# Moving the query and key transposes one unit ahead, and one mask ahead of an eviction, in a fused transformer block

## The chip, the cores and the metric

The kernel runs on one core of a Trainium2 chip. The metric is the time of one execution on the device in microseconds (us); the median of 14 runs of the kernel before is 694.04 us. A profile of one execution stands beside it. Engines are named as the profile does: PE (TensorE, matmuls and transposes), DVE (VectorE), ACT (ScalarE), POOL (GpSimd, here mostly indirect transfers), SP (SyncE, plain transfers).

## The reference

Input x has 8 sequences of 512 tokens with 128 features, all float32. Three residual steps follow each other:

```python
x = x + 0.5 * ffn(layernorm(x))     # 8 experts, 128 -> 512 -> 128, relu, the best 2 of 8 per token
x = x + attention(layernorm(x))     # 16 heads of 8, causal, rotary on some heads, decay on some
x = x + 0.5 * ffn(layernorm(x))     # the same weights again
```

Inside the attention, with q and k already rotated where a head's type asks for it:

```python
scores = einsum('bhqd,bhkd->bhqk', q, k) * dh ** (-0.5) + decay + causal
out    = einsum('bhqk,bhkd->bhqd', softmax(scores), v) @ w_o
```

## The kernel before

**Groups and units.** The attention is cut into 96 units, numbered 0 to 95: 8 sequences, each with 4 groups of 4 heads, each group with 3 units (`STEPS`, line 1227) that take key tiles 0; 1; and 2 with 3. Unit n therefore belongs to sequence n // 12, and n % 12 is its place there. In the trace, unit n begins with the n-th set of `st` matmuls (line 1238). The first attention unit starts at 143.4 us and the last at 558.9 us. Units below 0 and from 96 on carry only expert work and routing.

**What a unit does**, in `surround` (from line 1465), which writes the order out by hand for PE, ACT, DVE and SP:

1. `scores(n)`: PE computes the transposed scores of 4 heads into `st` (one PSUM buffer of four banks), and ACT takes the exponential in two halves of two heads each, `ee` (line 1245). The second `scores` can't begin before both halves of the one before are read.
2. `values(n - 1)`: PE multiplies the `ee` of the unit before with the values into `o` (line 1264). After a group's third unit ACT copies `o` to `oT`.
3. The first piece of expert work (below).
4. `causal(…, 0)`: DVE applies the mask to the first half of `ee` (line 1252), as a minimum with a tile that holds zeros and a very large number.
5. One queued transfer on POOL (`transfer`).
6. `outputs` in a group's second unit after the first group has ended: PE transposes `oT`, DVE takes the reciprocal of the sums (`recs`, line 1286) and writes `o_tok` (line 1287).
7. `causal(…, 1)`: the mask on the second half.
8. What is due in this unit (below), with further pieces between, then additions and a second transfer.

**Expert work.** Groups of tokens f0, f1, f2 (first expert step) and g0, g1, g2 (second) run beside the attention. A piece is one of three: a transpose of gathered rows (`xbT`, line 1000), a first layer part (`z`, line 1013, eviction to `h` at lines 1020 or 1022), or a second layer part (`y`, line 1037, eviction at line 1041, always DVE). A quota of one to three pieces goes into each unit. `m.evac` says which engine evicts the first piece of a unit if it is a transpose or a first layer part: DVE, but ACT in the places 8, 9 and 10 of a sequence, where DVE does the rotary work and writes `qpad` and `kpad` for the next sequence (lines 1193 to 1205). Later pieces of a unit are evicted by ACT.

**PSUM.** In the attention stage `st` and `o` have their own banks, and all else (pieces, transposes of queries, keys, outputs, normalised rows, qkv, routing) shares three banks called `m`: a new tile on PE waits until the old one in its bank is evicted.

**What is due.** `at(u, stream, steps)` puts steps of a generator into units u, u + 1, and so on; within a unit, they run in the order in which they were entered. For a sequence b that starts at unit u = 12 b:

- `operands(b, g)` has two steps. The first transposes the padded queries of group g (`qT_ps`, 4 transposes on PE) and copies them on DVE (`qT`). The second does the same for the keys (`kT_ps`), with the copy on ACT (`kT`, line 1221). `qT` and `kT` have two buffers each.
- `project(b + 1)` works in places 2 to 9 of sequence b: normalise (2 to 4), transpose (5), qkv matmuls with ACT's copies (6 and 7, lines 1176 to 1180), rotary (8), and `qpad`/`kpad` (9). So the first group's operands of the next sequence can't come before place 10.
- `finish(b)` and `route` of the sequence before come in places 2, 3 and from 4 on; `route` normalises in place 6 (line 774), transposes in 7 and computes the logits in 8.

**Transfers.** Scatters and gathers wait in a list; each, when issued on POOL, waits for the instruction that was last written down in `self.mark`: the latest mask of `causal` (line 1256) or the latest eviction of a first or second layer part (lines 1023 and 1044). The adds that use gathered rows are put two units after the gather (line 1120).

Of the kernel before, what the change touches and what calls it, by code (L numbers as in the profile page):

```python
# [1340 lines left out]
def macaron_kernel(  # L1341
# [24 lines left out]
    def run(*streams):  # L1366
        for s in streams:
            for _ in s:
                pass
# [12 lines left out]
    def take(stream, n):  # L1382

        for _ in range(n):
            if next(stream, STOP) is STOP:
                return
            yield
# [5 lines left out]
    with ExitStack() as main:  # L1393
        m = Main(tc, main, aps)
# [17 lines left out]
        def close(g):  # L1412
            m.close_group(g, order.index(g))

        def opened(g):

            pieces = m.experts(g)
            next(pieces)
            return pieces

        def step(*streams):
            for st in streams:
                next(st, None)

        def transfers(n):
            for _ in range(n):
                m.transfer()
# [4 lines left out]
        units = [(b, g, s) for b in range(B) for g in range(G) for s in range(len(m.STEPS))]  # L1432
        per = len(m.STEPS)
# [4 lines left out]
        def at(u, stream, steps, each=1):  # L1438

            for k in range(steps):  # L1440
                due.setdefault(u + k // each, []).append((stream, 1))

        def routed(u, shares, urgent=False, ahead=False):
            early = u < 0 or u > core
            r = m.route(shares, urgent, ahead, early)
            steps = 7 if early else 8
            if u > core:
                at(u, r, 3 + steps, 3)
                return
            if shares[0][0] is not f1:  # L1450
                at(u, r, 3)
                u += 3
            at(u, r, steps)

        def combined(u, g, i, dst=None, urgent=False, ahead=False):
            at(u, m.combine(g, i, dst, urgent, ahead), 1)
# [8 lines left out]
        def surround(n, att):  # L1465

            m.unit = n
            now = None
            for g, fetch, start, end in plan:
                if n == fetch:  # L1470
                    close(g)
                    fills[g.key] = [opened(g), g.pieces]
                if n == end:
                    run(fills[g.key][0])
                if start <= n < end:
                    now, until = fills[g.key], end
                    if g is g1 and att:
                        until = end + 7
            quota = min(now[1], -(-now[1] // (until - n))) if now else 0
            fill = now[0] if now else iter(())  # L1480
            if now:
                now[1] -= quota
            if att:
                ee = m.scores(*units[n])
            last, m.oT = m.oT, None
            if m.held is not None:
                got = m.values(*m.held)
                if got is not None:
                    m.oT = (*m.held[:2], got)
            m.held = (*units[n], ee) if att else None  # L1490
            m.evac = "dve" if att and n % seq not in (8, 9, 10) else "act"
            run(take(fill, 1 if quota else 0))
            m.evac = "act"
            if att:
                m.causal(units[n][2], ee, 0)
            m.transfer()
            if last is not None:
                m.outputs(*last)
            if att:
                m.causal(units[n][2], ee, 1)  # L1500
            if not att:
                m.additions()
            work = due.pop(n, [])
            todo = max(quota - 1, 0)
            for k, (stream, steps) in enumerate(work):
                some = todo // (len(work) - k + 1)
                run(take(stream, steps))
                run(take(fill, some))
                todo -= some
            if n >= core and len(m.jobs) + len(m.results) > 2:  # L1510
                run(take(fill, todo // 2))
                todo -= todo // 2
                m.transfer(second=True)
            run(take(fill, todo))
            m.additions()
            m.transfer(second=True)

        m.held = m.oT = None
        with m.banks(("m", 8)):

            n = [m.normalise(b) for b in range(5)]
            r = [m.route([(f0, 0)], early=True), m.route([(f0, 1)], early=True),
                 m.route([(f1, 0)], True, early=True)]
            step(n[0], n[0], n[1], n[1], n[0], n[0])
            step(r[0], n[1], n[1], r[0], r[1], r[0], r[0])
            transfers(8)
            step(r[1], r[1], r[1], n[2], n[2])
            transfers(8)
            step(n[3], n[3], n[4], n[4], *[r[0], r[1]] * 3, n[2], n[2])
            step(r[2], r[2], r[2], n[3], n[4], n[3], n[4])  # L1530
            run(*r[:2], *n)
            m.bias_columns()

            at(first, r[2], 4)
            routed(first + 1, [(f1, 1)], urgent=True)
            routed(first + 3, [(f1, 2)], urgent=True)
            routed(-22, [(f2, 0)], urgent=True)
            combined(-16, f0, 0, urgent=True, ahead=True)
            routed(-14, [(f2, 1)], urgent=True)
            combined(-12, f0, 1, urgent=True)  # L1540
            routed(-10, [(f2, 2)], urgent=True)
            at(-10, m.project(0), 8)
            for b in range(B):
                u = b * seq
                if b == 2:
                    combined(7, f1, 0, urgent=True, ahead=True)
                elif b > 2:
                    combined(u - (17 if b == 5 else 21), *place[True][b][0], urgent=b == 5, ahead=b == 5)
                if b > 0:
                    at(u - 10, m.project(b), 8)  # L1550
                for g in range(G):
                    at(u + g * per - 2, m.operands(b, g), 2)
                at(u + seq + 2, m.finish(b), 2, 2 if b == B - 1 else 1)
                routed(u + seq + (3 if b == B - 1 else 4), place[False][b], urgent=b in (1, 4, 5, 6, 7), ahead=b in (4, 6, 7))
            for i in range(2):
                combined(79 + 7 * i, g0, i, out)
            for i, (_, t0, t1) in enumerate(g1.shares):
                at(tail + 2 + 3 * i, m.collect(g1, i, out), 1 + t1 - t0)
            at(tail, m.verdict(bad), 2)

            for u in range(first, 0):
                surround(u, False)
                if u == first:
                    m.attention_constants()
                for _ in range(min(2, len(m.loads))):
                    m.loads.popleft()()
        with m.banks(("st", 1), ("o", 1), ("m", 3)):
            for u in range(core + 2):
                surround(u, u < core)
                if u >= 12 and m.later:  # L1570
                    m.later.popleft()()
        with m.banks(("m", 8)):
            for u in range(core + 2, ends):
                surround(u, False)
            run(fills["g2"][0])
            assert not due, due
            assert not m.jobs and not m.adds
            while m.results:
                m.transfer()
            last = [m.collect(g2, i, out, parts=min(2, g2.shares[i][2] - g2.shares[i][1])) for i in range(4)]  # L1580
            step(*last)
            run(*last)
# [53 lines left out]
```

## Time and profile before

| | |
|---|---|
| median of 14 runs | 694.04 us (691.68 to 695.62) |
| the profiled execution | 695.35 us, of which the span from first to last instruction is 693.6 us |
| mean granted TensorE clock | 0.978 |
| busy: PE, DVE, ACT, POOL | 623.1, 404.1, 347.2, 295.7 us |
| PE busy, 150 to 550 us, in stretches of 50 us | 50.00, 50.00, 49.51, 49.88, 48.58, 48.82, 46.58, 49.50 us |
| granted clock, 580 to 600 and 600 to 620 us | 0.83 and 0.83; 1.00 from 20 to 580 us |
| PE's longest waits outside the stage | for gathered rows, 9.9 us near the start; 3.4 us at 609.4 us |

In a timeline row the columns are start, length, engine, line, operation, output and input, shapes and count; a bracket gives how long the engine was idle just before, and whose work ended that. In a row of waits they are who waited for whom, the sum, how often, and the longest. PE's ends are modelled, so a wait is better read from the starts of the neighbours.

### The profile page before, as it was taken

To read this page: it belongs to the slowest core of one execution; us is meant where nothing else is said; L and a number is where in the kernel's file an instruction comes from. 1 tells how busy PE (TensorE), PEld (TensorE's weight loads), DVE (VectorE), ACT (ScalarE), POOL (GpSimd) and SP (SyncE) were. 2 spreads that over 40 slices of the span, in tenths; PEclk is the share of its full clock that TensorE was granted. 3 is DMA by queue.
4 is the path that set the end of the run, shared out by engine and by line. 5 is a ranking of instruction groups with operands and counts; after the bars stand their busy time and mean duration, and the time that the engine had idled before them with its cause. 6 is when DMAs were issued, how large, how long until landed. Compare 5 with 4: busy or idle time off the path is not lost. (4 is left out here: it accounts for less than half of the span.)

```text
span 693.6 us, 12921 instructions
## 1 busy us (share of the span) xinstructions
PE 623.1 (90%) x4797; PEld 403.5 (58%) x4797; DVE 404.1 (58%) x1426; ACT 347.2 (50%) x564; POOL 295.7 (43%) x318
## 2 busy tenths in 40 slices
PE   3259999999999999999999999999999998989980
PEld 2148867666556556555656656455565656747760
DVE  6736438735466665675676677777666554333423
ACT  4034443454755665466466565566646542234422
POOL 3744637643222214324054324342244556665550
PEclk9999999999999999999999999999999998989995
DMA  8746843313409941101211101012102121144225
GB/s 270 192 136 193 225 115 100 85 49 78 100 20 167 225 144 42 27 20 47 67 32 51 46 25 39 27 36 81 47 29 62 32 62 39 42 143 143 77 66 158
DMA packets 80230, 61.33 MB, mean 88 GB/s; under 512 B 7400, under 2 KB 73888, under 8 KB 80160
## 3 DMA queue, kind: packets, MB, share of 16 engines
q1 hardware_dynamic: 71296, 42.79, 24.0%
q0 software_dynamic: 8576, 17.63, 8.3%
q8 instruction: 40, 0.66, 0.4%
q14 instruction: 30, 0.25, 0.1%
q10 hardware_dynamic: 288, 0.01, 0.0%
HBM read 26.21 MB, written 34.19 MB: 87 GB/s over the span
## 5 line engine op out<-in xcount | busy, mean ns | idle before, releaser
L1245 ACT ACTIVATE ee<-st 128x768 f32<-128x768 f32 (+1 forms) x192 | 159.0, 881 | 90.5 <-PE st L1238 85.2
L479 POOL DMA_INDIRECT yt_f<-ys,back_f x64 | 65.1, 1018 | 128.7 <-DVE ee L1252 55.9
L1252 DVE TENSOR_TENSOR ee<-ee,keep 128x256 f32<-128x256 f32 (+1 forms) x192 | 93.2, 507 | 22.2 <-ACT ee L1245 21.9
L1037 PEld LDWEIGHTS y_f<-w_sb,h_f 128*120 128x120 f32 (+1 forms) x704 | 85.8, 182 | 28.5 <-issue 16.2
L1238 PE MATMUL st<-qT,kT 32*128 32x512 f32 (+3 forms) x1024 | 96.1, 467 | 5.7 <-ACT kT L1221 3.3
L1037 PEld LDWEIGHTS y_g<-w_sb,h_g 128*128 128x128 f32 x640 | 81.7, 193 | 32.5 <-issue 25.7
L895 POOL DMA_INDIRECT xs<-xn_g,to_g x64 | 63.8, 997 | 85.7 <-DVE ee L1252 32.5
L1037 PE MATMUL y_f<-w_sb,h_f 128*120 128x128 f32 (+1 forms) x704 | 93.9, 277 | 0.2 <-DVE h_f L1022 0.2
L1013 PE MATMUL z_g<-xT_g,w_sb 128*128 128x512 f32 (+1 forms) x192 | 91.0, 561 | 1.4 <-ACT xT_g L1004 1.4
L1264 PE MATMUL o<-ee,vpad 128*32 128x512 f32 (+3 forms) x1024 | 89.6, 442 | 0.8 <-DVE ee L1252 0.8
L1013 PE MATMUL z_f<-xT_f,w_sb 128*128 128x480 f32 (+1 forms) x192 | 88.9, 552 | 1.0 <-ACT xT_f L1004 1.0
L1020 ACT ACTIVATE h_f<-z_f,b1T 128x480 f32<-128x480 f32 (+1 forms) x86 | 53.5, 623 | 68.3 <-PE z_f L1013 67.4
L1037 PE MATMUL y_g<-w_sb,h_g 128*128 128x128 f32 x640 | 86.3, 280 | 0.5 <-DVE o_tok L1287 0.3
L981 POOL DMA_INDIRECT ys<-ysb_g,home_g x64 | 62.9, 983 | 51.6 <-ACT h_g L1020 17.0
L1020 ACT ACTIVATE h_g<-z_g,b1T 128x512 f32<-128x512 f32 (+1 forms) x77 | 49.4, 643 | 55.5 <-PE z_g L1013 55.3
L1041 DVE TENSOR_TENSOR ysb_f<-y_f,b_sb 120x128 f32<-120x128 f32 (+1 forms) x88 | 25.1, 288 | 77.7 <-PE y_f L1037 74.1
L1041 DVE TENSOR_TENSOR ysb_g<-y_g,b_sb 128x128 f32<-128x128 f32 x80 | 23.1, 290 | 79.4 <-PE y_g L1037 75.5
L1238 PEld LDWEIGHTS st<-qT,kT 32*128 32x128 f32 x1024 | 43.1, 183 | 39.0 <-ACT kT L1221 11.4
L895 POOL DMA_INDIRECT xs<-xn_n,to_f x40 | 39.1, 978 | 35.4 <-ACT xi_sb L732 8.3
L1264 PEld LDWEIGHTS o<-ee,vpad 128*32 128x32 f32 x1024 | 23.7, 108 | 52.5 <-issue 5.5
L1013 PEld LDWEIGHTS z_g<-xT_g,w_sb 128*128 128x128 f32 x192 | 30.5, 197 | 21.7 <-issue 12.5
L1013 PEld LDWEIGHTS z_f<-xT_f,w_sb 128*128 128x128 f32 x192 | 30.3, 194 | 13.9 <-issue 7.2
(187 smaller groups left out, 772.2 us busy)
## 6 DMA issues: line engine op xcount, KB each, us to landing
xs<-zeros SPq DMA_DIRECT2D x8, 520.0 KB
xb_g<-xs SPq DMA_DIRECT2D x16, 260.0 KB
w_sb<-in_L_ffn_W_dram SPq DMA_DIRECT2D x16, 256.0 KB
xb_f<-xs SPq DMA_DIRECT2D x16, 240.0 KB
ys<-ysb_f SPq DMA_DIRECT2D x16, 240.0 KB
ys<-zeros SPq DMA_DIRECT2D x2, 1664.0 KB
x<-in_L_attn_x_dram SPq DMA_DIRECT2D x8, 256.0 KB
xs<-zeros SPq DMA_DIRECT2D x1, 1920.0 KB
```

The costliest lines, as they stand in the source:

```text
L479: ins = op(*args, **kw)
L895: ins = nc.gpsimd.indirect_dma_start(out=g.xs[:, :], out_offset=bass.IndirectOffsetOnAxis(ap=to[:, t, r : r + 1], axis=0), in_=xn[:, t, : ...
L981: ins = nc.gpsimd.indirect_dma_start(out=g.ys[:, :], out_offset=bass.IndirectOffsetOnAxis(ap=home[e][:rows, t : t + 1], axis=0), in_=ys[:r ...
L1013: nc.tensor.matmul(z[:, :n], self.w1_sb[:, e, ts(c, P)], xT[:, n0 : n0 + n], start=True, stop=True,)
L1020: ins = nc.scalar.activation(dst, z[:, :n], AF.Relu, bias=bias)
L1037: nc.tensor.matmul(y[:rows], h[:, c, ts(t, rows)], self.w2_sb[:, e, c, :], start=(c == 0), stop=(c == C - 1),)
L1041: ins = nc.vector.tensor_tensor(ys[:rows, t, :], y[:rows], self.b2_sb[:rows, e], ALU.add)
L1238: nc.tensor.matmul(st[:, h, c0 : c0 + N - kt * P], kT[r0 : r0 + SLOT, ts(kt, P)], qT[r0 : r0 + SLOT, kt * P :], start=True, stop=True,)
L1245: nc.scalar.activation(ee[:, two, :width], st[:, two, :width], AF.Exp)
L1252: ins = self.nc.vector.tensor_tensor(d, d, self.keep.unsqueeze(1).unsqueeze(1).to_broadcast([P, 2, len(parts), P]), ALU.min,)
L1264: self.nc.tensor.matmul(self.o[h * SLOT : (h + 1) * SLOT, kt * P :], self.vpads[b % 2][:, kt, 4 * g + h, :], ee[:, h, c0 : c0 + n], start= ...
```

## The change

Two edits. In a sequence's groups 1 to 3 the operands are entered one unit ahead: queries in unit u + 3 g - 3 (the first unit of the group before) and keys in u + 3 g - 2 (its second), where they stood in the second and the third. The first group stays where it is. And the mask on the first half of `ee` is entered ahead of the first piece instead of behind it, so on DVE it stands in front of that piece's eviction; for the transfer that follows, the piece's eviction (if it sets the mark) is now the later mark.

```diff
             m.held = (*units[n], ee) if att else None
             m.evac = "dve" if att and n % seq not in (8, 9, 10) else "act"
+            if att:
+                m.causal(units[n][2], ee, 0)
             run(take(fill, 1 if quota else 0))
             m.evac = "act"
-            if att:
-                m.causal(units[n][2], ee, 0)
             m.transfer()
...
                 for g in range(G):
-                    at(u + g * per - 2, m.operands(b, g), 2)
+                    at(u + g * per - (3 if g else 2), m.operands(b, g), 2)
```

## The prediction

> **What bounds the kernel now.** I read the page's busy shares first, then PE's waits inside the attention stage (143 to 562 us, 96 units), then PE's, ACT's and DVE's timelines around those waits.
>
> The page's first part, and PE's waits between 143 and 562 us with one line of ACT's (us in total, times, longest):
>
> ```profile
> PE 623.1 (90%) x4797; PEld 403.5 (58%) x4797; DVE 404.1 (58%) x1426; ACT 347.2 (50%) x564; POOL 295.7 (43%) x318
> ...
> PE st L1238 <- ACT kT L1221: 3.3, 8, 0.7
> PE st L1238 <- ACT ee L1245: 1.5, 3, 0.6
> PE qkv_ps_a L1176 <- DVE o_tok L1287: 1.4, 4, 0.7
> ...
> ACT ee L1245 <- PE st L1238: 85.2, 85, 4.3
> ```
>
> PE sets the pace: ACT waits for PE's scores 85 times, while PE waits for others a few us in all. So only what shortens PE's waits counts. The view's own waits are measured from modelled matmul ends; I therefore size a wait from starts: the time from the start of one group of matmuls to the start of the next, less the smallest such time for the same pair (four transposes take 0.44). The kT wait, unit 69, and the exponential wait behind it, PE then ACT:
>
> ```profile
> 446.00 0.63 PE L1215 MATMUL kT_ps<-ident,kpad 128*128 128x128 f32 x4
> 447.31 1.14 PE L1238 MATMUL st<-qT,kT 32*128 32x512 f32 x8 [0.68 <-ACT kT L1221]
> 448.38 0.86 PE L1264 MATMUL o<-ee,vpad 128*32 128x256 f32 x16
> 449.17 0.70 PE L1013 MATMUL z_g<-xT_g,w_sb 128*128 128x256 f32 x2
> 450.51 0.93 PE L1238 MATMUL st<-qT,kT 32*128 32x384 f32 x8 [0.64 <-ACT ee L1245]
> ...
> 446.67 0.59 ACT L1221 COPY kT<-kT_ps 128x512 f32<-128x512 f32 x1 [1.61 <-PE kT_ps L1215]
> 448.52 1.94 ACT L1245 ACTIVATE ee<-st 128x1024 f32<-128x1024 f32 x2 [1.26 <-PE st L1238]
> ```
>
> Transposes at 446.00, copy from 446.67 to 447.26, scores at 447.31: 1.31 us where 0.44 would do, so 0.87 lost.
>
> **Keys and queries sooner.** Nothing is added: 24 groups' two sets of transposes (0.44 each on PE), the qT copy on DVE (0.68) and the kT copy on ACT (0.59) move one unit ahead; no DMA moves. Read from starts, scores wait for kT seven times in groups 1 to 3: 0.30 (st at 350.24), 0.36 (372.88), 0.30 (399.81), 0.40 (432.98), 0.87 (447.31), 0.89 (468.91), 0.21 (480.01), together **3.33 gained**. The waits of first groups (0.42, 0.30, 0.87 at 361.31, 410.89, 457.94) stay. What is late next is the exponentials of the unit before: they ended 0.94 to 2.25 us ahead of those seven scores; less the wait and less the 0.44 of transposes that leave that unit, 0.10 and 0.04 are left at 432.98 and 468.91, 0.75 or more elsewhere, so they stay just hidden. In the unit that receives the qT transposes, the scores of unit 73 (461.14) wait 0.81 for exponentials; 0.44 of that is now filled: **0.44**.
>
> The seventh unit of a sequence (n%12 = 7) loses qT's copy from DVE and gets kT's on ACT. Unit 31, PE, then DVE, then ACT:
>
> ```profile
> 289.25 0.66 PE L1215 MATMUL qT_ps<-ident,qpad 128*128 128x128 f32 x4
> 290.17 1.75 PE L1176 MATMUL qkv_ps_a<-wqkv_sb,xnT_a 128*128 128x384 f32 x4 [0.26 <-DVE o_tok L1287]
> 291.76 1.06 PE L1037 MATMUL y_f<-w_sb,h_f 128*120 128x128 f32 x8
> ...
> 288.48 0.72 DVE L1022 TENSOR_SCALAR h_f<-z_f,b1T 128x480 f32<-128x480 f32 x1 [2.41 <-PE z_f L1013]
> 289.11 0.42 DVE L1252 TENSOR_TENSOR ee<-ee,keep 128x256 f32<-128x256 f32 x1
> 289.44 0.25 DVE L1286 RECIPROCAL recs<-otok_ps 128x16 f32<-128x16 f32 x1
> 289.73 0.29 DVE L1287 TENSOR_TENSOR o_tok<-otok_ps,recs 128x128 f32<-128x128 f32 x1
> ...
> 291.09 0.37 ACT L1179 COPY qkv_a<-qkv_ps_a 128x256 f32<-128x256 f32 x1 [3.07 <-PE qkv_ps_a L1176]
> ```
>
> From transposes to the piece behind qkv: 2.51 us. The third qkv matmul group needs the bank that o_tok frees, and the piece needs the bank that the ACT copies free. With the first mask done early, recs and o_tok come 0.33 sooner (mask start to recs start); in the built program of the changed kernel the fourth qkv matmul then waits for kT's copy, 0.67 + 0.59 + about 0.13 = 1.39 after the transposes start, and the piece comes 0.65 later: 2.04, or 0.47 gained. Unit 7's kin, 19, 43, 55, 67, 79, take 2.19, 2.31, 2.38, 2.47, 2.98 now and by the same steps 2.04 (79: 2.36, as DVE writes home rows first), which gives 0.15, 0.27, 0.34, 0.43, 0.62. Unit 7 itself has 0.32 behind the same copies (take 0.30), unit 91 has 0.48 behind o_tok (take 0.33). Together **2.91**.
>
> Against it: in the sixth unit qT now stands in front of qkv. In the built program the piece behind qkv gets the bank of the first qkv matmul, which ACT must empty: 0.92 from matmul to copy, 0.54 to the end of both copies, 0.13, that is 1.59 against 1.32 unhindered, as at 290.17 to 291.76. Units 18, 30 and 54 have such a piece: 3 x 0.28 = **0.85 lost**. Had the piece taken qT's bank, it would wait for DVE's mask, four normalisations (1.11) and the copy: about 1.3 each, 3.9 in all; I take 0.85 because the built program names the bank, and keep 3.9 for the range.
>
> DVE is full in units 8 to 10, and there some gain is given back. In unit 70, DVE then PE:
>
> ```profile
> 452.47 0.42 DVE L1202 TENSOR_SCALAR qpad<-qkv_a 128x512 f32<-128x512 f32 x1
> ...
> 453.33 0.60 PE L1215 MATMUL qT_ps<-ident,qpad 128*128 128x128 f32 x4
> ```
>
> The next sequence's transposes need qpad, ready 0.44 before. PE gains 0.87 + 0.44 (kT's wait and its transposes) + 0.43 by then; following DVE's unbroken run from the logits on, qpad comes only 1.1 sooner: 0.65 lost; in unit 58 (slack 0.14) the same reading gives 0.30. **0.95 lost.**
>
> **The mask in front.** The same masks, another order, in 72 units whose first piece DVE evicts (if not, ACT does, and DVE's order stays). The mask waits for the first exponential; queued behind it are the eviction, recs and o_tok, and behind these PE's banks. I compared in every such unit the eviction's start with the first exponential's end plus the mask (0.42, or 0.69 in a group's third unit): the eviction would be late in 16 of 72, by 0.04 to 0.38, 1.96 in sum. A piece's bank is asked for again three banks later, over 1.5 us, so I take 0 of it and keep 1.96. The last unit gains: DVE, unit 95:
>
> ```profile
> 561.25 0.69 DVE L1006 COPY xT_g<-xbT_ps_g 128x512 f32<-128x512 f32 x1 [1.30 <-PE xbT_ps_g L1000]
> ...
> 562.33 1.29 DVE L1252 TENSOR_TENSOR ee<-ee,keep 128x512 f32<-128x512 f32 x2
> ```
>
> Its exponentials ended at 560.73 and 561.43, yet both masks run from 562.33 to 563.62, and PE's values wait. With the first mask at 560.8 the second ends near 563.1 and the values 0.7 sooner: **0.70**.
>
> That the masks stood there with their input ready shows a queue served in order. The Trainium skill, PSUM — Partial Sum Buffer, section Engine vs sequencer instructions, calls VectorE's queue strict FIFO, which speaks against a mask that may wait at its head; the rows agree on the order, and by the rule alone all 1.96 would be paid.
>
> The mask is also a marker: a unit's first POOL transfer waits for whichever of mask and piece came last. In most units that now is DVE's eviction, some 0.3 sooner. In units 8 to 10 the eviction is ACT's behind both exponentials, some 0.9 later (unit 32: mask over at 295.3, eviction at 296.16); 16 of those 24 units have such a piece. The adds that use a gather come two units (8 us) later, and no DVE wait on a gather is in the list: 0.
>
> **Sum.** 3.33 + 0.44 + 2.91 + 0.70 - 0.85 - 0.95 = 5.58; for waits of the size of 0.1 that I did not follow I take off 0.5: 5.1. The profiled execution took 695.35 (span 693.6 and 1.75 around it), so 690.3; it lay 1.3 over the median 694.04, so the forecast is 688.9. What follows the attention, the last sequence's routing and its experts, hangs on the last values and shifts with them.
>
> **Rivals.** *DVE takes over*: if units 8 to 10 run at DVE's pace in every sequence, what is gained in units 7 to 9 (2.91 and the 0.30, 0.30 and 0.87 of the kT waits) goes, 0.95 is counted already: 5.1 - 4.38 + 0.95 = 1.7, 692.4. For it: two cases above; against: in the others DVE waits for exponentials inside unit 9 (0.27 to 0.49 each). *The exponentials take kT's place*: the 3.33 goes, 692.3; against it the margins above. *The held eviction* (the FIFO rule): 1.96 back, 690.9; for it 16 units, against it the three banks. *Transfers behind the later mark, slower*: if the 0.9 in those 16 units reached PE through late rows, 14.4 - 5.1 = 9.3, 703.3; from six such units on the change loses. Against it: the 8 us, and that PE waits for no fetched rows inside the stage. That nothing moves is no case: the built orders differ as told.
>
> **Numbers.** Forecast 0.58, DVE takes over 0.15, held eviction 0.08, exponentials 0.08, transfers 0.07, others, such as one slowed stretch of PE's clock more or fewer after the attention (granted 0.83 over 580 to 600 and again over 600 to 620, 3.4 us each), 0.04. A measurement here tells 0.2%, 1.4 us, from no change. Faster: 0.57 + 0.10 + 0.07 + 0.05 = 0.79; slower 0.07 + 0.02 = 0.09; same 0.12. The range goes from 686.2 (no loss paid: 7.4, and run spread) to 693.0, which takes in both rivals near 692 and qT's bank at 3.9.
>
> **What would show it.** Right: the st waits for kT fall to the three of first groups; qkv's third matmul group starts within 0.2 of its transposes' end; 0.3 appears behind qkv in units 18, 30, 54; the last values end some 5 us sooner than their 564.45. Wrong: st waits on ee in more than four places, idle PE before qT with qpad as releaser, or DVE waits on gathers.

## The result and the profile after

The changed kernel took 688.62 us (median of 10 runs, 686.87 to 689.59), the kernel before 694.18 (47 runs, 691.49 to 696.6): ratio 0.9918, 95% interval 0.9905 to 0.993, that is 5.6 us faster. The profiled execution after took 687.75 with a span of 686.0. All these runs are from one chip, called A below; the experiments ran on B and C, where the kernel before took 707 to 710, and what that difference taught is part of what follows. (The record numbers B and C, 7 and 13, but not A; that A is a third chip is taken from the times.) Ratios are of undisturbed runs, so they need not be the quotient of the medians beside them.

The page's first part of after, PE's waits from 143 to 562 us (sum, times, longest), DVE's first wait there, and the masks' group (busy, mean ns; idle before, releaser):

```profile
PE 621.1 (91%) x4797; PEld 403.9 (59%) x4797; DVE 411.3 (60%) x1426; ACT 348.7 (51%) x564; POOL 295.0 (43%) x318
...
PE st L1238 <- ACT kT L1221: 1.1, 3, 0.7
PE st L1238 <- ACT ee L1245: 1.1, 3, 0.6
...
PE qkv_ps_a L1176 <- DVE o_tok L1287: 0.4, 1, 0.4
PE o L1264 <- DVE ee L1252: 0.3, 1, 0.3
...
DVE ee L1252 <- ACT ee L1245: 91.2, 83, 3.8
...
L1252 DVE TENSOR_TENSOR ee<-ee,keep 128x256 f32<-128x256 f32 (+1 forms) x192 | 97.9, 511 | 91.8 <-ACT ee L1245 91.2
```

The waits for kT fell from eight to the three of first groups. DVE now stands 91.2 us in front of a mask, against 21.9 before, yet PE waits for a mask only once, 0.3: DVE used to stand in front of the piece instead (its waits for y fell from 67.9 us to 26.7).

I call the time from a unit's first `st` matmul to the next unit's its length. Lengths repeat to 0.01 between profiles where nothing else intervenes, so they size single terms far below what a median can tell. Two things do intervene on chips B and C: exponentials that start late, and stretches of halved clock; both are told below. From the first unit's start to the last one's the stage took 415.47 before and 409.81 after.

The seventh unit that the prediction worked through, unit 31, after: PE, DVE, ACT.

```profile
289.35 0.66 PE L1215 MATMUL kT_ps<-ident,kpad 128*128 128x128 f32 x4
289.93 1.67 PE L1176 MATMUL qkv_ps_a<-wqkv_sb,xnT_a 128*128 128x384 f32 x4
291.43 1.04 PE L1037 MATMUL y_f<-w_sb,h_f 128*120 128x128 f32 x8
...
287.45 0.42 DVE L1252 TENSOR_TENSOR ee<-ee,keep 128x256 f32<-128x256 f32 x1 [1.44 <-ACT ee L1245]
288.58 0.72 DVE L1022 TENSOR_SCALAR h_f<-z_f,b1T 128x480 f32<-128x480 f32 x1 [0.70 <-PE z_f L1013]
289.21 0.25 DVE L1286 RECIPROCAL recs<-otok_ps 128x16 f32<-128x16 f32 x1
289.49 0.29 DVE L1287 TENSOR_TENSOR o_tok<-otok_ps,recs 128x128 f32<-128x128 f32 x1
```

The mask runs 1.1 us ahead of the piece's eviction, o_tok comes 0.14 after the transposes' start instead of 0.48, qkv follows the transposes after 0.58 instead of 0.92, and the piece behind qkv stands 2.08 after the transposes (2.51 before).

The end of the stage, DVE then PE:

```profile
554.89 0.69 DVE L1252 TENSOR_TENSOR ee<-ee,keep 128x512 f32<-128x512 f32 x1 [0.80 <-ACT ee L1245]
555.50 0.68 DVE L1006 COPY xT_g<-xbT_ps_g 128x512 f32<-128x512 f32 x1
...
556.57 0.68 DVE L1252 TENSOR_TENSOR ee<-ee,keep 128x512 f32<-128x512 f32 x1
...
557.31 0.84 PE L1264 MATMUL o<-ee,vpad 128*32 128x256 f32 x12 [0.33 <-DVE ee L1252]
558.08 1.16 PE L1037 MATMUL y_g<-w_sb,h_g 128*128 128x128 f32 x8
```

The first mask is early, the second isn't: it stands behind the eviction and three small instructions. From the last unit's start to the piece behind the last values it took 5.03, against 5.53 before.

### The profile page after: what moved, and what is told of

Its sections match the earlier page's. It is cut to its first block, busy times and chain, and to the rows that moved or that the text cites. A ratio compares the mean times of both kernels' runs of the same rounds, so it can differ in the third digit from the quotient of the medians.

```text
span 686.0 us, 12913 instructions
## 1 busy us (share of the span) xinstructions
PE 621.1 (91%) x4797; PEld 403.9 (59%) x4797; DVE 411.3 (60%) x1426; ACT 348.7 (51%) x564; POOL 295.0 (43%) x318
## 5 line engine op out<-in xcount | busy, mean ns | idle before, releaser
L1252 DVE TENSOR_TENSOR ee<-ee,keep 128x256 f32<-128x256 f32 (+1 forms) x192 | 97.9, 511 | 91.8 <-ACT ee L1245 91.2
L1264 PE MATMUL o<-ee,vpad 128*32 128x256 f32 (+3 forms) x1024 | 89.9, 442 | 0.4 <-DVE ee L1252 0.3
```

What stands on the lines that cost most here:

```text
L1252: ins = self.nc.vector.tensor_tensor(d, d, self.keep.unsqueeze(1).unsqueeze(1).to_broadcast([P, 2, len(parts), P]), ALU.min,)
L1264: self.nc.tensor.matmul(self.o[h * SLOT : (h + 1) * SLOT, kt * P :], self.vpads[b % 2][:, kt, 4 * g + h, :], ee[:, h, c0 : c0 + n], start= ...
```

## The experiments

Theory A, going in: the kT waits and the seventh units carry the gain, the seventh units through the earlier mask. The rivals were the operands alone, and the held eviction. The first four kernels ran on chip B (before: 706.89), the others on chip C (before: 709.67 and 708.16 in its two groups). Neither the whole change nor the kernel before was profiled on chip B, so the lengths of the first four are compared with chip A's profiles.

**Operands alone.**

```diff
-                    at(u + g * per - 2, m.operands(b, g), 2)
+                    at(u + g * per - (3 if g else 2), m.operands(b, g), 2)
```

> Queries and keys one unit sooner, the mask left behind the first piece. Theory A (the gain of the seventh units hangs on the mask, through recs and o_tok, which free the bank of a qkv matmul): the waits of scores on kT go (3.0) and unit 73 gains its 0.44, but the seventh units gain 0.3 in all instead of 2.8, because qkv still starts about 0.9 after its transposes (0.92 in unit 31 before, 0.58 after); the sixth units lose 0.7, DVE's pace in units 8 to 10 some 0.2. Sum 2.8 faster than before: about 691.3, 2.7 slower than the whole change. The values of the last unit gain nothing. Rival B (the seventh units gain because kT's copy by ACT stands where qT's copy by DVE stood): 3.0 + 0.44 + 2.4 - 0.7 - 0.4 = 4.7 faster, about 689.4.

Measured 705.12, ratio 0.997 (0.9937 to 1.0004). The interval takes in no change as well as theory A's 2.8 faster, so the lengths decide. By lengths, the units that lose a kT wait are as short as in the whole change (unit 68: 3.53 against 4.76 before), and the last values gain nothing (5.53). The seventh units gained 1.49, neither 0.3 nor 2.4. Unit 31 of it:

```profile
295.12 0.66 PE L1215 MATMUL kT_ps<-ident,kpad 128*128 128x128 f32 x4
296.04 1.53 PE L1176 MATMUL qkv_ps_a<-wqkv_sb,xnT_a 128*128 128x384 f32 x4 [0.26 <-DVE o_tok L1287]
297.40 1.04 PE L1037 MATMUL y_f<-w_sb,h_f 128*120 128x128 f32 x8
```

qkv still starts 0.92 behind the transposes, for o_tok, as theory A has it; but from there to the piece it takes 1.36 instead of 1.59, because kT's copy on ACT is over by then. Both halves count.

**Mask alone.**

```diff
             m.evac = "dve" if att and n % seq not in (8, 9, 10) else "act"
+            if att:
+                m.causal(units[n][2], ee, 0)
             run(take(fill, 1 if quota else 0))
             m.evac = "act"
-            if att:
-                m.causal(units[n][2], ee, 0)
```

> The first mask in front of the first piece's eviction, queries and keys where they were before. Theory A: in the seventh units o_tok comes 0.33 sooner and then qT's copy on DVE is the next limit, ready 1.50 after the transposes instead of 1.41 for kT's copy on ACT; they gain 2.1 in all, the last values 0.5, together 2.6 faster than before: about 691.5. The three kinds of score waits on kT stay (3.3 in 8 places by PE's waits). Rival B (operands carry the seventh units): 0.5 faster only, 693.6. Rival C (held eviction, a queue served strictly in order pays for every wait of the mask at its head): 2.6 - 2.0 = 0.6 faster, 693.5, and PE would then show waits on DVE's evictions (h, xT, ysb) that the kernel before does not have; B and C are told apart by the seventh units' lengths in the trace.

Measured 709.72, ratio 1.0038 (1.0012 to 1.0065): slower, where theory A had 2.6 faster. The seventh units did gain 1.91, close to theory A's 2.1, so rival B can't be the whole account of them. But units 11, 29, 47, 53, 65, 74 and 86, where nothing was expected, grew by 0.48 to 1.38 each, and PE's waits show DVE's evictions. That is rival C, in a few units, and with a cause that chip A's profiles don't have: in those units the first exponential starts 0.4 to 1.6 us later behind its scores than the 1.0 of chip A. Units 53, 65 and 74 grow in the kernel before too, as its profile on chip C shows below, so their growth isn't all the mask's. Unit 48 grew most, by 1.58, and not through its exponential: the granted clock was 0.50 from 366.90 to 370.31, over most of this unit, soon after PE had waited 1.68 for h_g in unit 47. In the second profile of the same kernel unit 48 has its 3.38 of before.

**Keys alone one unit sooner** (both steps in the second unit of the group before).

```diff
-                    at(u + g * per - (3 if g else 2), m.operands(b, g), 2)
+                    at(u + g * per - 2, m.operands(b, g), 2, 2 if g else 1)
```

> The whole change, but of groups 1 to 3 only the keys go one unit ahead; the queries stay, so both sets of transposes stand in the same unit (places 1, 4 and 7). Theory A: the kT waits go as in the whole change (3.0), but unit 73 loses its 0.44 again, the sixth units get back the 0.7 of their bank, and the seventh units carry both copies and one set of transposes more in front of qkv: o_tok, qT's copy on DVE and kT's copy on ACT hold all three shared banks, qkv waits for each in turn, and each of the 8 pays 0.5 or more beside the 0.44 that it gets and the sixth unit loses. Sum against the whole change: 4 + 0.44 - 0.7 = 3.7 slower, about 692.3. Rival: the move of the queries is worth nothing by itself (0.44 - 0.7), seventh units are no longer than one more set of transposes: about 688.4.

Measured 708.05, ratio 1.0016 (0.9991 to 1.004): no gain over the kernel before, where theory A had 1.9 faster. In the places 0, 1, 3, 4, 6 and 7, which have few late exponentials, its lengths sum to 3.44 more than the whole change's on chip A (theory A: 3.7): the seventh units alone are 6.14 longer, of which 3.5 are the moved transposes, and the places 1 and 4 lose 0.6 and 0.7 beyond theirs. So the queries' move is worth what the units with both sets of transposes would else lose, the seventh above all, not the 0.44 of unit 73.

**First groups too**: queries and keys both in place 10.

```diff
-                    at(u + g * per - (3 if g else 2), m.operands(b, g), 2)
+                    at(u + g * per - (3 if g else 2), m.operands(b, g), 2, 1 if g else 2)
```

> The whole change, and the first group of each sequence has queries and keys both in place 10 (keys stood in place 11). Theory A: the last three waits of scores on kT (0.42, 0.30 and 0.87 by starts in the kernel before) go, 1.1 to 1.6; kpad is written right behind qpad (0.42 each) and PE waits about 0.4 for it where qpad is already the limit, as in unit 70, so some 0.3 to 0.8 comes back: about 1 faster than the whole change, 687.6. Rival (DVE sets the pace in units 8 to 10 of every sequence, and keys would wait for kpad each time): seven sequences at 0.4 to 0.6 cost 3 to 4, less 1.1 to 1.6: about 2 slower, 690.6.

Measured 700.34, ratio 0.9898 (0.986 to 0.9936). No wait of scores on kT is left among PE's waits. What the first groups add to the whole change is told by lengths alone: against its profile on chip A the units of place 10 are 3.64 longer, those of place 11 5.54 shorter, unit 12 0.17 longer: 1.7 gained, where 1 was expected.

**The whole change, the mask in two places, the mask alone once more, and the kernel before**, on chip C. The second differs from the whole change in this:

```diff
-            if att:
+            early = n % seq == 7 or n == core - 1
+            if att and early:
                 m.causal(units[n][2], ee, 0)
             run(take(fill, 1 if quota else 0))
             m.evac = "act"
+            if att and not early:
+                m.causal(units[n][2], ee, 0)
```

> The changed kernel itself, beside the others of this group. On the chip of the first profiles 5.6 faster (ratio 0.992). The chip of the runs with one part of the change alone took 13 us more for the kernel before, and there the first exponential of a third unit started up to 1.7 us late in 8 to 12 units. Theory A: where that happens the mask at the head of DVE's queue holds the first piece's eviction and PE loses 0.5 to 1.4 in each such unit, so the gain is 2 to 4 on that chip and 5.6 on one without. Rival: the lateness costs the kernel before as much, and the gain is 5 to 6 on either.

> The whole change, but the mask goes in front of the first piece's eviction in place 7 of each sequence and in the last unit alone; in the other units it stays behind. Theory A (the mask's gain is made in those nine units: 1.3 to 1.9 in place 7 and 0.5 at the end): every unit as long as in the whole change within 0.05 where exponentials are on time, so the same time within 0.3 on a chip without late exponentials, and 2 to 4 faster than the whole change on one with them. Rival (the mask also helps elsewhere, by o_tok and the banks it frees): slower than the whole change by 0.5 or more.

> The mask alone once more, beside the whole change on one chip. Theory A: undisturbed units gain 1.9 in place 7, and the last values 0.5, so 2.4 faster than before where exponentials are on time; where they are late as in the first run of it, each such unit gives back 0.5 to 1.4, and it is 1 to 3 slower than before. Rival (held eviction everywhere): slower than before on either chip, with PE waiting for DVE's evictions in units whose exponentials are on time.

> The kernel before, for its profile on this chip. Theory A: where its exponentials are late, its pieces are evicted all the same (the mask stands behind them), and such a unit grows by less than 0.3. Rival: its units grow by the same 0.5 to 1.4 as with the mask in front.

Measured: whole change 705.91, ratio 0.9959 (0.9928 to 0.999), 2.9 faster than before; mask in two places 703.24, 0.991 (0.9879 to 0.9942), 6.4 faster; mask alone 711.61, 1.0052 (1.0024 to 1.0079), 3.7 slower; the kernel before 708.12 in its one run. Unit 47 shows how the early mask can cost. The whole change: PE, ACT, DVE, POOL.

```profile
365.84 0.94 PE L1238 MATMUL st<-qT,kT 32*128 32x256 f32 x16
367.49 0.70 PE L1013 MATMUL z_g<-xT_g,w_sb 128*128 128x256 f32 x2
370.58 0.44 PE L1000 MATMUL xbT_ps_g<-ident,xb_g 128*128 128x128 f32 x2 [1.79 <-DVE h_g L1022]
...
368.59 0.81 ACT L1245 ACTIVATE ee<-st 128x768 f32<-128x768 f32 x1 [3.94 <-PE pos_ps_g L869]
...
369.43 0.69 DVE L1252 TENSOR_TENSOR ee<-ee,keep 128x512 f32<-128x512 f32 x1 [2.20 <-ACT ee L1245]
370.04 0.48 DVE L1022 TENSOR_SCALAR h_g<-z_g,b1T 128x256 f32<-128x256 f32 x1
...
365.32 1.02 POOL L479 DMA_INDIRECT yt_f<-ys,back_f  x1 [0.30 <-issue]
366.85 0.94 POOL L479 DMA_INDIRECT yt_f<-ys,back_f  x1 [0.50 <-issue]
```

The kernel before, the same unit on the same chip:

```profile
363.16 0.94 PE L1238 MATMUL st<-qT,kT 32*128 32x256 f32 x16
364.81 0.70 PE L1013 MATMUL z_g<-xT_g,w_sb 128*128 128x256 f32 x2
366.09 0.44 PE L1000 MATMUL xbT_ps_g<-ident,xb_g 128*128 128x128 f32 x2
...
364.16 1.51 ACT L1245 ACTIVATE ee<-st 128x768 f32<-128x768 f32 x2 [2.19 <-PE st L1238]
...
365.55 0.48 DVE L1022 TENSOR_SCALAR h_g<-z_g,b1T 128x256 f32<-128x256 f32 x1 [1.25 <-PE z_g L1013]
365.95 1.28 DVE L1252 TENSOR_TENSOR ee<-ee,keep 128x512 f32<-128x512 f32 x2
...
362.13 0.95 POOL L479 DMA_INDIRECT yt_f<-ys,back_f  x1 [0.84 <-DVE ee L1252]
363.92 0.94 POOL L479 DMA_INDIRECT yt_f<-ys,back_f  x1 [0.84 <-DVE x L1098]
```

PE starts its matmuls at the same distances in both (z 1.65 behind the scores). In the whole change the exponential comes 2.75 behind the scores instead of 1.00; z has long been ready, but DVE stands at the mask, h_g is evicted behind it at 370.04, and PE waits 1.79 for h_g's bank. (The exponential reads the scores alone. Its bracket names pos_ps because releasers are inferred from the time of the release, which was late; for the late exponentials of units 11 and 29 in the same profile the bracket names `o`.) PE's waits in the mask-alone run name the same pair, between 145 and 570 us:

```profile
PE xbT_ps_g L1000 <- DVE h_g L1022: 1.8, 1, 1.8
PE y_g L1037 <- DVE h_g L1022: 1.6, 2, 1.4
PE y_f L1037 <- DVE h_f L1022: 1.1, 2, 0.8
```

How seven units with late exponentials grew, each against the same program (or the one that it must equal there) on chip A:

| unit | before | mask alone | whole change | mask in two places |
|---|---|---|---|---|
| 11 | 0 | 0.53 | 0.56 | 0 |
| 29 | 0 | 0.89 | 0 | 0 |
| 38 | 0.39 | 0.34 | 0 | 0 |
| 47 | 0 | 1.47 | 1.49 | 0 |
| 53 | 0.49 | 1.54 | 0.68 | 0.69 |
| 65 | 0.25 | 0.61 | 1.78 | 1.21 |
| 74 | 0.59 | 0.49 | 0.79 | 0.66 |

With the mask behind the piece a late exponential costs nothing in 11 and 29 (it comes 0.8 late there in the kernel before), and in 47 it is on time; in 38, 53, 65 and 74 it costs in either order, and in 38, 53 and 74 the expectation of less than 0.3 for the kernel before failed. The price of the early mask on such a chip is thus partly the held eviction and partly, as in unit 47, that the exponential itself comes late in this order alone. Units 0 and 66 of the whole change's profile grew too, by 1.38 and 1.34, but a stretch of 3.4 us at a granted clock of 0.50 lies over each, so they are not in the table.

Unit 65, the largest growth of the table, is mainly a price of the earlier keys and not of the mask: with the operands alone on chip B it grew by 1.12. The scores behind it, in the kernel before and in the whole change:

```profile
439.20 1.14 PE L1238 MATMUL st<-qT,kT 32*128 32x512 f32 x8 [0.24 <-ACT kT L1221]
...
443.85 1.74 PE L1238 MATMUL st<-qT,kT 32*128 32x512 f32 x8 [1.70 <-ACT ee L1245]
```

On chip A the exponentials stay hidden in front of these scores by 0.20 only. Here the first of them comes 1.9 late and PE waits for it instead of for kT: in this unit the prediction's rival, the exponentials taking kT's place, came true.

From the kernel before to the whole change's later profile on chip C (its run further below, with no halved clock in the stage) the stage became 3.09 shorter, against 5.66 on chip A. Of the 2.57 between them unit 47 makes 1.44, unit 65 0.80 and unit 11 0.57; the rest cancel to less than 0.3.

The times make it likely that the mask in two places is faster than the whole change on this chip, 2.7 by medians, but their ratios' intervals overlap. By lengths it saves 2.0 in units 11 and 47 and loses some of it elsewhere, and its stage, 414.49, is no shorter than the 414.15 of the whole change's later profile.

The mask in two places also shows where else the mask counts. Its unit 70 is 4.36 long, as with the operands alone (4.37), against 3.76 in all three profiles of the whole change. DVE around units 68 to 70, and PE's values of unit 69:

```profile
451.93 0.29 DVE L1041 TENSOR_TENSOR ysb_g<-y_g,b_sb 128x128 f32<-128x128 f32 x1 [3.04 <-PE y_g L1037]
452.14 1.28 DVE L1252 TENSOR_TENSOR ee<-ee,keep 128x512 f32<-128x512 f32 x2
...
457.44 1.30 PE L1264 MATMUL o<-ee,vpad 128*32 128x512 f32 x8 [0.70 <-DVE ee L1252]
```

The same place in the whole change on chip A:

```profile
441.84 0.69 DVE L1252 TENSOR_TENSOR ee<-ee,keep 128x512 f32<-128x512 f32 x1 [2.04 <-ACT ee L1245]
442.84 0.29 DVE L1041 TENSOR_TENSOR ysb_g<-y_g,b_sb 128x128 f32<-128x128 f32 x1 [0.30 <-PE y_g L1037]
443.05 0.68 DVE L1252 TENSOR_TENSOR ee<-ee,keep 128x512 f32<-128x512 f32 x1
...
447.76 1.30 PE L1264 MATMUL o<-ee,vpad 128*32 128x512 f32 x8
```

Unit 68 is in place 8, but its first piece is a y, which DVE evicts everywhere. With the mask in front DVE works while it would wait for y, and starts its long run through the routing and rotary work 0.6 earlier; behind it, unit 69's masks come late and PE waits 0.70 for them. The rival of that run was right in this unit. Units 75 and 87 are longer too than in the whole change on chip A, by 0.52 and 0.21, as they are with the operands alone (0.52 and 0.14); the cause there was not followed.

**First groups too, queries behind qkv, and both**, each on top of the mask in two places. The second:

```diff
                 if b > 0:
                     at(u - 10, m.project(b), 8)
+                    at(u - 6, late, 1)
                 for g in range(G):
-                    at(u + g * per - (3 if g else 2), m.operands(b, g), 2)
+                    ops = m.operands(b, g)
+                    if g == G - 1 and b < B - 1:
+                        late = ops
+                        at(u + g * per - 2, ops, 1)
+                    else:
+                        at(u + g * per - (3 if g else 2), ops, 2)
```

> The mask in front in place 7 and the last unit alone, and each sequence's first group with queries and keys both in place 10. By the first run with first groups in place 10, units 10 to 12 together became 1.7 shorter than in the whole change. Theory A: 1.7 faster than the run with the mask in two places, whose ratio was 0.991: 0.9885, and 2 to 5 faster than the whole change on the same chip. Rival (DVE sets the pace in units 8 to 10, the first eviction there is ACT's, and kpad holds the keys): no faster than the mask in two places, 0.991.

> The mask in two places as before, and in place 6 the queries' transposes stand behind the two qkv matmul groups instead of in front of them. The piece behind still needs the bank of the first of these, but 0.44 of transposes now lie between. Theory A (the 0.25, 0.25 and 0.20 of units 18, 30 and 54 are that bank's wait): these three units end at 0.44 over the kernel before instead of 0.69, 0.69 and 0.64, and all else stays: 0.7 faster than the mask in two places in the sum of units, too little for the times to tell (ratio 0.990). Rival (the wait is for qkv's own input or for PE work in that unit): no unit changes.

> All three together: mask in front in place 7 and the last unit, first groups in place 10, queries behind qkv in place 6. Theory A: the terms add, 1.7 + 0.7 = 2.4 faster than the mask in two places alone, ratio 0.9875, and 3 to 6 faster than the whole change on this chip. Rival (the gain of the first groups is taken back in units 8 to 12 by DVE's pace): 0.990.

> The whole change beside the three variants, on their chip. Theory A: 2 to 4 faster than before if third units' exponentials are late on this chip, 5 to 6 if they are on time. Rival: 5 to 6 on either.

Measured: 701.93, ratio 0.992 (0.9893 to 0.9946); 702.55, 0.9924 (0.9895 to 0.9953); 701.42, 0.9911 (0.988 to 0.9941); the whole change 706.12, 0.9971 (0.9949 to 0.9992), 2.0 faster than before. Lengths: with the first groups too, the units of places 10 and 11 are together 1.5 shorter than with the mask in two places, and units 12, 48 and 72 together 0.5 longer, so 1.0 is gained where 1.7 was expected; queries behind qkv give 5.46 in units 18 and 30 (0.44 over the kernel before, as expected; 5.71 in the whole change) and 4.49 in 54 (4.64), and lose 0.36 in unit 78. Unit 30 of it, PE:

```profile
290.78 1.45 PE L1176 MATMUL qkv_ps_a<-wqkv_sb,xnT_a 128*128 128x384 f32 x4
292.07 0.60 PE L1215 MATMUL qT_ps<-ident,qpad 128*128 128x128 f32 x4
292.51 1.04 PE L1037 MATMUL y_f<-w_sb,h_f 128*120 128x128 f32 x8
```

qkv to transposes takes 1.29, transposes to the piece 0.44, so nothing waits. The three variants can't be told from each other or from the mask in two places by their times. First groups too and all three together were expected at 0.9885 and 0.9875; both figures lie below the measured intervals, while the rivals' 0.991 and 0.990 lie inside. These two do lie below the whole change with intervals that don't meet: on chip C they beat both kernels. The whole change with the first groups and the mask everywhere wasn't run on chip C (on chip B it had 0.9898), so how much of that is the mask's place is not shown. They weren't run on chip A, where lengths give the mask in two places no advantage (unit 70 would lose 0.6). The mask in front in place 8 as well was not tried.

## Why the prediction was right, point by point

| term | predicted | measured on chip A, by lengths |
|---|---|---|
| seven kT waits | +3.33 | +3.00 |
| queries in unit 73's wait | +0.44 | +0.44 |
| seventh units | +2.91 | +2.81 |
| last values | +0.70 | +0.51 |
| first qkv's bank in units 18, 30, 54 | -0.85 | -0.70 |
| DVE's pace, units 70 and 58 | -0.95 | -0.41 |
| waits not followed | -0.5 | +0.52 |
| sum | 5.1 | 6.2 |

The sum is the stage's 5.66 and the last values' 0.51; the row of waits not followed is what the other rows leave of it. The medians differ by 5.6; the half us between is within the spread of single runs (689.59 - 686.87 = 2.7 after). That the forecast, 688.9, came so near to 688.62 is partly luck: terms taken 0.6 too high and terms taken 1.7 too low stand against each other.

- **Keys sooner.** Right in kind and nearly in size on chip A: 0.27, 0.36, 0.26, 0.31, 0.79, 0.80 and 0.21 came back in units 44, 50, 56, 65, 68, 74 and 77. The exponentials behind stayed hidden by little where the text said so: 0.20 and 0.14 are left at the scores of units 66 and 75 (predicted 0.10 and 0.04).
- **Seventh units.** The steps held: qkv early through the mask, then kT's copy as the limit; 2.08 measured in unit 31 where 2.04 was worked out. The two runs with one half each gained 1.49 and 1.91, together more than 2.81: the mask and the exchange of copies take away two waits of which either alone uncovers part of the other.
- **The bank in the sixth units.** The named bank was the right one (0.25, 0.25, 0.20), and the run with the queries behind qkv took the loss away to the hundredth in units 18 and 30.
- **DVE's pace.** Right in cause, wrong in the wait, and mis-sized, 0.95 for 0.41. In unit 70 the transposes follow their neighbours in the usual 0.44, qpad being ready in time. What comes late is a step earlier: the values wait for unit 69's masks, 1.04 behind the scores against 0.86 before. In the size two errors work against each other, and a third adds to it. "If not, ACT does, and DVE's order stays" failed: unit 68's first piece is a y, which DVE evicts in every place, so the mask moved there too and DVE started its run earlier. Without it unit 70 loses 1.0, as three runs show, where the reading along DVE's run had given 0.65; with it, 0.40. And unit 58, taken at 0.30, lost 0.01, with the operands alone too.
- **Last values.** Mis-sized, 0.51 for 0.70. The second mask ends at 557.25, just where the prediction had it (563.1 less the 5.86 by which the last unit came sooner), and the piece follows 0.83 behind it in both kernels. But from 563.62 to 563.1 is 0.52, so the 0.70 did not follow from its own step.
- **Waits not followed.** The 0.5 taken off was wrong in sign: units 14, 29, 53 and 86 gave 0.68 more, under 0.2 each, and little was lost elsewhere (0.20 in unit 0).
- **The mask's held evictions and the transfers at zero.** Right on chip A: with 91.2 us of DVE standing at the mask, no wait of PE on an eviction was added. The rule that the prediction weighed (the Trainium skill, PSUM — Partial Sum Buffer, Engine vs sequencer instructions: VectorE's queue is strictly first in, first out) gives the order, which all runs show; what the order costs hangs on how long the head waits. On chip A no wait of PE came of it; on chips B and C the head waited up to 1.9 longer and the rule was paid in some units: mask alone 2.7 and 3.7 slower than before. On chip C, the only other one where the whole change ran, the forecast of 5.1 would have been 2 to 3 too high (2.0 and 2.9 measured).

## What to carry to other kernels

Put an instruction that waits for a late engine in front of one that is ready only where the order is known to help (here nine units, and unit 68), not everywhere because it costs nothing in one profile: the slack behind it is what absorbs a late producer. On two chips the early mask by itself made the kernel slower; that fewer early masks beat the whole change is seen in units 11 and 47 and made likely, not shown, by the times. Size a term by the time from one start to the next in the same place of two profiles, which repeats to 0.01 us, and test a sum of small terms that way when the medians can't part them. When something is moved on a queue, list every kind of work that can stand in that place, also the rare ones.

## What the runs showed of the hardware that was not expected

On chips B and C the release of the scores in a group's third unit (16 small `st` matmuls), read as the start of its first exponential, often came late, by up to 1.9 us, although PE's later matmuls started at their usual distances. It goes with POOL: in the twelve profiles of the two chips there are 384 third units. In the 143 where POOL issued no indirect transfer during the first 0.95 us of the scores, 2 first exponentials came more than 0.12 late; in the 119 where it issued for 0.5 us or more of that time, 109 did, by 0.8 in the median; of the 122 in between, 78 did. In chip A's two profiles none of 21 such units was late. Unit 47 above is one case: with the early mask a transfer runs from 365.32 to 366.34, over the scores of 365.84, and the release is late; in the kernel before it ends at 363.08, ahead of the scores of 363.16, the next begins 0.76 behind them, and the release is on time. This is a coincidence of times, shown many times over, and no kernel without transfers was run: whether POOL's issuing holds back PE's releases on two chips, and why not on the third, stays open. If POOL is the cause, one term of the prediction, transfers at zero, holds for chip A alone. The late releases are at most a small part of why the kernel before takes 13 to 15 us more on the others: its stage is 1.8 longer on chip C. The rest lies ahead of the stage (it starts 5 us later) and behind it, where the second stretch of halved clock lasted 13.7 us in the profile of the kernel before on chip C and 6.8 on chip A.

On these chips the granted clock was also halved at times inside or at the start of the stage, for 3.41 us each: from 366.90 in the first mask-alone profile, 0.84 behind the end of a wait of PE of 1.68; from 444.3 in the first of the whole change, 0.4 behind one of 1.70; and from 150.7 there and 148.9 in the profile of all three together, at the first unit's scores, which had waited 2.85 and 2.16. The unit underneath grew by 1.3 to 1.6 each time, so a held engine can cost more than its wait. Waits of 1.79 in unit 47 and of 2.6 at the stage's start of the whole change's later profile were not followed by such a stretch; what decides it stays open.
